# First-phase loads issued one by one behind pieces of the second transform, and five of the last image's tile pairs added by VectorE

## The chip, the cores and the metric

One core of a Trainium2 chip runs the whole program. The metric is the device time of one execution in microseconds, as the median of several runs. A profiled execution is one further run, with its own time. The engines are called PE (TensorE, the matrix engine), PEld (its weight loads), DVE (VectorE), ACT (ScalarE), POOL (GpSimd) and SP (SyncE, which only issues DMA transfers here).

## The reference, cut to what matters

The input `x` has 32 images of 128 channels by 64 x 64 pixels in float32. Three layers follow each other:

```python
x = x + conv(group_norm(x))            # a convolution through 2-D butterfly transforms:
                                       #   transform, product with the transformed weights, transform back
t = to_tokens(x)                       # 32 x 4096 tokens of 128 channels
t = t + attention(layer_norm(t))       # for each image softmax(K^T V) over its 4096 tokens, 128 x 128
t = t + moe(layer_norm(t))             # 8 experts, the best two by router weight, gates renormalised
x = from_tokens(t)
```

In `conv`, `group_norm` has groups of four channels, so every image needs its mean and variance over all 4096 pixels before its transform. In `moe`, each token's result is the sum over experts of gate times expert output; the gates of six of the eight experts are zero, and the kernel computes all eight and weighs them.

## The kernel before, in words

The program has three phases, and one image, or one column of frequencies, at a time goes through each.

**First phase** (about 0 to 980 us): norm and forward transform. Image `b` is loaded in eight pieces of 128 x 512 by SP (`load`, L307), then DVE takes statistics of each piece (`stats`, L315) and joins them (L324). A short exchange between PE (L328, L338), DVE (L333 to L341) and POOL gives the group's mean and the reciprocal of its deviation: POOL's power is L345. From image 4 on DVE then norms the image in four pieces (L358); for the first four images ACT does it (L356). PE transposes the image in four groups, called `pz` (L369), and ACT copies them out (L379). PE multiplies along the width in eight groups, `pv` (L392), and ACT copies (L403). PE multiplies along the height in eight groups, `pf` (L414); the copies `fo` out of the accumulator (L424) are DVE's, except those of groups 3 and 7, which are ACT's. SP stores each copy with two transfers (L432) to the tensor `xf` in HBM. There are three buffers for images (`x`), four accumulators in PSUM for all of `pz`, `pv` and `pf` (`ps`), and four buffers for copies on their way to HBM (`f`).

These stages are pipelined. In the slot `s` of the loop PE does, in turn, pieces of `pz` of image `s`, of `pv` of image `s-1` and of `pf` of image `s-2`.

The order on every engine is written out ahead of time by a small planner, the class `Plan`. Each piece of work is added with an engine, an estimated duration, a due time, what it comes after and which buffers it takes and frees. The planner plays this through, and whenever an engine is free it takes the ready piece with the smallest due time. The order found in this way is the order in which the instructions are issued; each engine then works strictly in that order and waits where data or buffers aren't ready. PE's order in the first phase is that of the code. In the calls of `add`, the due time is in slots of 27.5 us. For the loads it reads:

```python
for k in range(8):
    add(("x", b, k), "SP", 0.45, b - 2 + 0.1 * k, load(b, k), [("pz", b - 3, g) for g in range(4)],
        ("x",) if k == 0 else (), (), 4.0)
for k in range(4):
    add(("bn", b, k), "DVE", 1.4, at + 0.02 * k, stats(b, k), [("x", b, 2 * k), ("x", b, 2 * k + 1), ("nm", b - 2, 3)])
```

So all eight loads of an image become ready when image `b - 3` has been transposed, and one piece of statistics takes two pieces of the image.

The small butterfly matrices of the transforms are built in the same phase (`butterfly`): matrix 1 by DVE at the start, matrices 0 and 2 by POOL during slots 3 to 8, in six levels (`level`, L216 to L222) that each wait for the one before. Their twiddle factors come by SP (L187). `select` (L244 to L250) is a further small piece on POOL. In slots 12 to 15 POOL arranges the weights (L277, L282), PE transposes them (L293) and DVE copies them (L298).

**Second phase** (about 980 to 2650 us): product with the weights, column by column; the change does not touch it.

**Third phase** (about 2650 us to the end): inverse transform, attention and experts, again planned, with one image's experts running beside the next images' earlier stages. An image has 32 tiles of 128 tokens (`NT`), treated in 16 pairs. For each tile and each half of the experts PE makes four experts' outputs, 128 x 512 in one accumulator (`expert`, L1200, three accumulators `pe`). DVE multiplies them by the gates into a tile `tm` (`gated`, L1211); there are two tiles `tm`, one for each pair on its way. POOL adds a pair's sixteen products (`summed`): two additions of 128 x 512 (L1222), one more of the same size (L1223) and two onto the tokens `t` (L1225). PE then transposes four finished tiles back (`back`, L1232), ACT copies (L1238) and SP stores (L1239). For the last image nothing else is left to run beside this. Just before it, DVE works out that image's gates (L1108 to L1152).

Of the kernel before, what the change touches and what calls it, by code (L numbers as in the profile page):

```python
# [12 lines left out]
ALU = mybir.AluOpType  # L13
# [3 lines left out]
P = 128  # L17
# [73 lines left out]
def kernel(  # L91
# [15 lines left out]
    nc = tc.nc  # L107
    B = x.shape[0]
# [11 lines left out]
    pf = dram.tile([n, n, P * n], F32, name="pf")  # L120
# [37 lines left out]
    with ExitStack() as ph1:  # L158
# [9 lines left out]
        made, xs, zs, vs, tile_of = {}, {}, {}, {}, {}  # L168
        on_pe = []

        def add(key, engine, us, at, run, after=(), take=(), free=(), late=0.0):
            after = [made[k] for k in after if k in made]
            if engine == "PE":
                after += on_pe[-1:]
            made[key] = plan.add(engine, us, SLOT * at, run, after, take, free, late)
            if engine == "PE":
                on_pe.append(made[key])
# [5 lines left out]
        def twiddles(m):  # L183
            def run():
                t = tile_of["tw", m] = bp.tile([P, 6, 2, 2, 2, n // 2], F32, tag="tw", name=f"tw{m}")
                for ax in range(2):
                    nc.sync.dma_start(  # L187
                        t[ax * n : (ax + 1) * n].rearrange("p a i j c d -> p (a i j c d)"),
                        tw[m, ax].rearrange("a i j c d -> (a i j c d)").partition_broadcast(n),
                    )  # L190
            return run
# [111 lines left out]
        def load(b, k):  # L303
            def run():
                if k == 0:
                    xs[b] = xp.tile([P, NPIX], F32, tag="x", name=f"x{b}")
                nc.sync.dma_start(xs[b][:, k * 512 : (k + 1) * 512], xv[b][:, k * 512 : (k + 1) * 512])  # L307
            return run

        def stats(b, k):  # L310
            def run():
                if k == 0:
                    tile_of["bs", b] = st.tile([P, 8, 6], F32, name=f"gbs{b}", tag="gbs", bufs=2)
                for j in range(2 * k, 2 * k + 2):
                    nc.vector.bn_stats(tile_of["bs", b][:, j, :], xs[b][:, j * 512 : (j + 1) * 512])  # L315
            return run

        def group_norm(b):
# [116 lines left out]
        def butterfly(m, engine, eng, at, us):  # L435

            before = {1: [], 0: [("b1", 5), "wi", ("nm", 4, 3)], 2: [("b0", 5), "wd"]}[m]
            add(("tw", m), "SP", 0.9, -3.0 if m == 1 else at - 0.3, twiddles(m), before, (), (), 4.0)
            add((f"b{m}", -1), engine, 2 * us / 7, at, unit(m, eng), before)
            for idx in range(6):  # L440
                add((f"b{m}", idx), engine, us, at + 0.01 * idx, level(m, idx, eng), [("tw", m), (f"b{m}", idx - 1)])

        def norm(b):

            at = b - 1
            for k in range(8):
                add(
                    ("x", b, k), "SP", 0.45, b - 2 + 0.1 * k, load(b, k), [("pz", b - 3, g) for g in range(4)],
                    ("x",) if k == 0 else (), (), 4.0,
                )  # L450
            for k in range(4):
                add(("bn", b, k), "DVE", 1.4, at + 0.02 * k, stats(b, k), [("x", b, 2 * k), ("x", b, 2 * k + 1), ("nm", b - 2, 3)])

        def norm_on_pe(b, step):
            if not 0 <= b < B:
                return
            at = b - 0.9
            if step == 0:
                gn = tile_of["gn", b] = group_norm(b)
                add(("ag", b), "DVE", 0.4, at, gn[0], [("bn", b, k) for k in range(4)])  # L460
                add(("g1", b), "PE", 0.3, at, gn[1], [("ag", b)], ("ps",))
                add(("gm", b), "DVE", 0.7, at, gn[2], [("g1", b)])
            else:
                gn = tile_of.pop(("gn", b))
                add(("g2", b), "PE", 0.3, at, gn[3], [("gm", b)])
                add(("gr", b), "DVE", 0.25, at, gn[4], [("g2", b)], (), ("ps",))
                add(("gp", b), "POOL", 0.6 if b >= 4 else 1.6, at, gn[5], [("gr", b)])
                for k in range(4):
                    add(("nm", b, k), *(("DVE", 0.85) if b >= 4 else ("ACT", 1.05)), at + 0.01 * k, gn[6][k], [("gp", b)])
# [34 lines left out]
        norm_on_pe(0, 0)  # L504
        norm_on_pe(0, 1)
        for s in range(B + 2):
            if s + 2 < B:
                norm(s + 2)
            for g in range(4):
                at = s + 0.25 * g  # L510
                if g == min(s, 3) - 1:
                    norm_on_pe(s + 1, 0)
                piece("pz", s, g, at)
                for k in range(2):
                    piece("pv", s - 1, 2 * g + k, at + 0.04 + 0.04 * k)
                if g == min(s, 3) - 1:
                    norm_on_pe(s + 1, 1)
                for k in range(2):
                    piece("pf", s - 2, 2 * g + k, at + 0.12 + 0.07 * k)
            if s == 0:  # L520
                norm_on_pe(1, 0)
                norm_on_pe(1, 1)
            if s == 3:
                butterfly(0, "POOL", nc.gpsimd, 3.2, 4.5)
                add("sel", "POOL", 2.5, 3.5, select, [("nm", 4, 3)])
            if s == 6:
                add("wr", "PE", 0.6, 6.0, weight_rows, [("b0", 5), "sel"], ("ps",))
                add("wd", "DVE", 0.8, 6.0, weight_matrices, ["wr"], (), ("ps",))
                butterfly(2, "POOL", nc.gpsimd, 7.0, 4.5)
                add("wo", "DVE", 1.2, 9.0, output_matrices, [("b2", 5)])  # L530
                add("wm", "SP", 0.5, 10.0, weight_taps, [("b2", 5)], (), (), 4.0)
            if 12 <= s < 16:
                k = s - 12
                add(("wr", k), "POOL", 5.0, s - 0.5, onto_rows(k), ["wm", ("pf", s - 3, 4)], ("f",))
                add(("wt", k), "PE", 1.1, s, rows_turned(k), [("wr", k)], ("ps",))
                add(("we", k), "DVE", 1.25, s, rows_out(k), [("wt", k)], (), ("ps", "f"))
# [4 lines left out]
    with ExitStack() as ph2:  # L541
# [11 lines left out]
        made, tile_of = {}, {}  # L553
# [614 lines left out]
    def experts(b):  # L1168
# [37 lines left out]
        def gated(i, half):  # L1206
# [8 lines left out]
                )  # L1215
            return run

        def summed(j):
            def run():
                tm, lo = tile_of.pop(("tm", b, j)), 2 * j  # L1220
                for k in range(2):
                    nc.gpsimd.tensor_tensor(tm[:, k, 0:4, :], tm[:, k, 0:4, :], tm[:, k, 4:8, :], ALU.add)  # L1222
                nc.gpsimd.tensor_tensor(tm[:, :, 0:2, :], tm[:, :, 0:2, :], tm[:, :, 2:4, :], ALU.add)  # L1223
                for m in range(2):
                    nc.gpsimd.tensor_tensor(t[:, lo : lo + 2, :], t[:, lo : lo + 2, :], tm[:, :, m, :], ALU.add)  # L1225
            return run
# [16 lines left out]
        for g in range(8):  # L1243
            at = s2 + 0.125 * g
            add(b, f"xn{g}", "ACT", 1.7, at - 0.1, normal(g), ["nb"], ("xn",))
            add(b, f"px{g}", "PE", 0.55, at - 0.05, turn(g), [f"xn{g}"], ("tl", "xT"), ("xn",))
            add(b, f"xT{g}", "ACT", 0.6, at - 0.05, turned(g), [f"px{g}"], (), ("tl",))
            for k in range(4):
                i = 4 * g + k
                for half in range(2):  # L1250
                    add(
                        b, f"pe{i}_{half}", "PE", 0.86, at + 0.125 * (2 * k + half) / 8, expert(i, half), [f"xT{g}"],
                        ("pe",), ("xT",) if k == 3 and half else (),
                    )
                    add(
                        b, f"m{i}_{half}", "DVE", 0.7, at + 0.125 * (2 * k + half) / 8, gated(i, half),
                        [f"pe{i}_{half}", "gt"] + ([f"m{i - k % 2}_0"] if k % 2 or half else []), ("tm",) if k % 2 == 0 and half == 0 else (),
                        ("pe",) + (("gate",) if i == NT - 1 and half else ()),
                    )
                if k % 2:  # L1260
                    add(
                        b, f"s{i // 2}", "POOL", 5.45, at + 0.125 * (2 * k + 2) / 8, summed(i // 2),
                        [f"m{i - 1 + a}_{h}" for a in range(2) for h in range(2)], (), ("tm",),
                    )
            add(b, f"st{g}", "PE", 0.55, at + 0.25, back(g), [f"s{2 * g}", f"s{2 * g + 1}"], ("tl",))
            add(b, f"so{g}", "ACT", 0.6, at + 0.25, store(g), [f"st{g}"], (), ("tl",))
# [61 lines left out]
```

## Time and profile before

| what | us |
|---|---|
| median of 3 runs (lowest to highest) | 6242.58 (6241.29 to 6246.91) |
| the profiled execution's own time | 6250.6 |
| its span from first to last instruction | 6248.9 |
| PE busy | 6005.3 (96%) |
| DVE busy | 4200.0 (67%) |
| ACT busy | 3757.1 (60%) |
| POOL busy | 4205.2 (67%) |
| first phase's slots of images 3 to 30 | 824.0, PE busy 783.3 |
| last image's sums on POOL | 6158.1 to 6243.8 |

The page is one profiled execution. Busy time counts instructions at work on an engine; an engine that waits in front of an instruction isn't busy. PE's time is the sum of matrix instructions, with weight loads (PEld) beside it. "Idle before" says how long an engine stood before an instruction and what ended that. The granted clock is the rate that the chip allowed PE, as a share of full speed. Times with a decimal point in the timelines are counted from the start of the span.

### The profile page before, as it was taken

How to read it: one execution, taken by the hardware profiler on the slowest of the kernel's cores; microseconds unless marked ns; L12 is line 12 of the kernel's file. 1: busy time of each engine (PE TensorE's matmuls, PEld its weight loads, DVE VectorE, ACT ScalarE, POOL GpSimd, SP SyncE). 2: the span in 40 equal slices, each digit the busy share in tenths (PEclk: the TensorE clock that was granted, in tenths of full speed). 3: DMA queues.
4: the chain of work that ended last, by engine and by line, in shares of the span. 5: the costliest groups of instructions: out<-in, count | busy, mean ns of one | idle time of the engine just before them, and what ended most of it. 6: DMA issues, size and time to landing. Idle time of an engine off the chain costs nothing. (4 is left out here: it accounts for less than half of the span.)

```text
span 6248.9 us, 218347 instructions
## 1 busy us (share of the span) xinstructions
PE 6005.3 (96%) x94922; PEld 4726.7 (76%) x94922; DVE 4200.0 (67%) x7626; ACT 3757.1 (60%) x7089; POOL 4205.2 (67%) x3780
## 2 busy tenths in 40 slices
PE   7999999999999999889999999999999999999987
PEld 7899998999999999766666666666666666666653
DVE  5555544555555555347878787787878778787876
ACT  6666664555555555466666676667667666766652
POOL 2110005666666666328888888888888888888889
PEclk9999999999999999899999999999999999999999
DMA  5666656666666666622222122222313222221100
GB/s 201 215 216 210 231 192 190 175 171 170 173 174 170 171 172 174 170 77 85 77 67 95 62 93 67 85 78 65 95 62 93 68 85 76 68 94 62 64 21 24
DMA packets 556965, 756.55 MB, mean 121 GB/s; under 512 B 58466, under 2 KB 321892, under 8 KB 551908
## 3 DMA queue, kind: packets, MB, share of 16 engines
q1 hardware_dynamic: 554096, 741.38, 39.7%
q8 instruction: 745, 12.21, 0.9%
q14 instruction: 216, 1.77, 0.1%
q10 hardware_dynamic: 1908, 1.19, 0.1%
HBM read 406.80 MB, written 335.54 MB: 119 GB/s over the span
## 5 line engine op out<-in xcount | busy, mean ns | idle before, releaser
L1200 PE MATMUL pe<-ew_sb,xT 128*128 128x512 f32 x4096 | 1982.4, 601 | 53.2 <-DVE tm L1211 52.8
L1211 DVE TENSOR_TENSOR tm<-pe,oh 128x512 f32<-128x512 f32 x2048 | 1353.4, 684 | 563.4 <-PE pe L1200 419.0
L1222 POOL TENSOR_TENSOR tm<-tm 128x512 f32<-128x512 f32 x1024 | 1306.7, 1291 | 313.1 <-DVE tm L1211 260.7
L1200 PEld LDWEIGHTS pe<-ew_sb,xT 128*128 128x128 f32 x4096 | 691.1, 191 | 523.4 <-issue 327.8
L623 PE MATMUL m<-f,s 128*64 128x64 f32 x32768 | 1070.1, 224 | 6.3 <-POOL s L574 4.6
L612 DVE COPY f<-g 128x1024 f32<-128x1024 f32 x512 | 626.9, 1224 | 664.5 <-PE g L601 664.5
L623 PEld LDWEIGHTS m<-f,s 128*64 128x64 f32 x32768 | 999.1, 138 | 68.3 <-POOL s L574 4.9
L574 POOL COPY s<-l 128x512 f32<-128x512 f32 x512 | 546.9, 1103 | 596.7 <-issue 516.4
L612 ACT COPY f<-g 128x1024 f32<-128x1024 f32 x512 | 518.6, 1013 | 576.6 <-PE g L601 549.3
L1225 POOL TENSOR_TENSOR tk<-tk,tm 128x256 f32<-128x256 f32 x1024 | 759.4, 742 | 80.3
L839 ACT COPY u<-pu 64x512 f32<-64x512 f32 x1024 | 593.5, 580 | 313.7 <-PE pu L829 302.8
L1223 POOL TENSOR_TENSOR tm<-tm 128x512 f32<-128x512 f32 x512 | 652.4, 1274 | 40.2
L829 PEld LDWEIGHTS pu<-qw,r 128*128 128x128 f32 x4096 | 507.2, 198 | 169.1 <-ACT u L839 91.5
L601 PE MATMUL g<-c,wst 9*128 9x128 f32 x16384 | 608.0, 284 | 4.7 <-ACT f L612 3.5
L829 PE MATMUL pu<-qw,r 128*128 128x128 f32 x4096 | 526.2, 284 | 62.5 <-ACT u L839 55.4
L345 POOL TENSOR_TENSOR grstd<-gms,mhalf 128x1 f32<-128x1 f32 x32 | 17.7, 553 | 790.0 <-DVE gms L341 752.8
L601 PEld LDWEIGHTS g<-c,wst 9*128 9x128 f32 x16384 | 509.3, 187 | 40.7 <-ACT f L612 4.5
L414 PE MATMUL pf<-ph,v 128*128 128x128 f32 x4096 | 497.4, 280 | 22.3 <-issue 15.9
L576 POOL TENSOR_SCALAR s<-l 128x512 f32<-128x512 f32 x256 | 510.3, 1993 | 0.0
L414 PEld LDWEIGHTS pf<-ph,v 128*128 128x128 f32 x4096 | 471.9, 193 | 33.8 <-issue 17.4
L1238 ACT COPY so<-po 128x512 f32<-128x512 f32 x256 | 150.9, 589 | 572.7 <-issue 413.1
L884 DVE BATCH_NORM_STATS2 bs<-tk 128x6 f32<-128x128 f32 x2048 | 447.9, 279 | 57.0 <-ACT tk L915 44.9
(165 smaller groups left out, 8486.1 us busy)
## 6 DMA issues: line engine op xcount, KB each, us to landing
xf<-f SPq DMA_DIRECT2D x512, 256.0 KB, 3.9
l<-xf SPq DMA_DIRECT2D x1024, 128.0 KB, 3.3
pf<-o SPq DMA_DIRECT2D x1024, 128.0 KB, 3.2
r<-pf SPq DMA_DIRECT2D x512, 256.0 KB, 4.7
x<-in_x_dram SPq DMA_DIRECT2D x256, 256.0 KB, 5.4
y<-in_x_dram SPq DMA_DIRECT2D x32, 2048.0 KB, 8.2
out_dram<-so SPq DMA_DIRECT2D x256, 256.0 KB, 2.0
tw<-in_tw_dram SPq DMA_DIRECT2D x6, 384.0 KB, 6.0
```

Of the source, the lines that this page charges most:

```text
L414: nc.tensor.matmul(pl[:, j * P : (j + 1) * P], vs[b][:, 8 * g + j, :], ph.rearrange("h r m -> h (r m)"), start=True, stop=True,)
L574: nc.gpsimd.tensor_copy(dst, src)
L601: nc.tensor.matmul(pg[g // 2][:, g % 2, m * P : (m + 1) * P], wst[rows, 16 * half + 4 * t + m, :], c[rows].rearrange("r h k -> r (h k)"), ...
L612: copy(f.rearrange("i m (g o) -> i m g o", g=2), tile_of["g", w, half, t][k].rearrange("i g (o m) -> i m g o", o=4))
L623: nc.tensor.matmul(ps[hh * n : (hh + 1) * n, q, :], s[:, h].rearrange("i k b -> i (k b)")[:, B * r : B * r + n], f[:, h, r, :], start=(r = ...
L829: nc.tensor.matmul(ps[:, k, :], rs[b, e][:, k * P : (k + 1) * P], qw.rearrange("w r m -> w (r m)"), start=True, stop=True,)
L839: nc.scalar.copy(u[r * n : (r + 1) * n, :, oh * n + 8 * e : oh * n + 8 * e + 8], ps[oh * n : (oh + 1) * n, :, r * n : (r + 1) * n].rearran ...
L1200: nc.tensor.matmul(ps, tile_of["xT", b, i // 4][:, i % 4, :], ew_sb[:, es, :].rearrange("d e c -> d (e c)"), start=True, stop=True,)
L1211: nc.vector.tensor_tensor(tile_of["tm", b, i // 2][:, i % 2, es, :], tile_of.pop(("pe", b, i, half)).rearrange("p (e c) -> p e c", c=P), t ...
L1222: nc.gpsimd.tensor_tensor(tm[:, k, 0:4, :], tm[:, k, 0:4, :], tm[:, k, 4:8, :], ALU.add)
L1223: nc.gpsimd.tensor_tensor(tm[:, :, 0:2, :], tm[:, :, 0:2, :], tm[:, :, 2:4, :], ALU.add)
L1225: nc.gpsimd.tensor_tensor(t[:, lo : lo + 2, :], t[:, lo : lo + 2, :], tm[:, :, m, :], ALU.add)
```

## The change

In the first phase, the statistics are added to the plan piece by piece, eight for an image, each after the one before. From image 4 on, load `k` of image `b` comes after load `k - 1` and after piece `k` of the height transform `pf` of image `b - 4`, and is added to the plan inside the loop over the slot's groups. The butterflies on POOL, but not their twiddle loads, get a due time later by 99 slots, and `select` gets the due time 99.

In the third phase, for the last image alone, five of the sixteen tile pairs (3, 6, 9, 12 and 15) are neither multiplied into `tm` nor added by POOL. Instead DVE takes each expert's output from the accumulator, multiplies it by the gate of the token and adds it onto `t` with one instruction per expert: four for each half, sixteen for a pair.

```diff
@@ stats
-                for j in range(2 * k, 2 * k + 2):
-                    nc.vector.bn_stats(tile_of["bs", b][:, j, :], xs[b][:, j * 512 : (j + 1) * 512])
+                nc.vector.bn_stats(tile_of["bs", b][:, k, :], xs[b][:, k * 512 : (k + 1) * 512])
@@ butterfly
             add(("tw", m), "SP", 0.9, -3.0 if m == 1 else at - 0.3, twiddles(m), before, (), (), 4.0)
+            at += 99 if engine == "POOL" else 0
             add((f"b{m}", -1), engine, 2 * us / 7, at, unit(m, eng), before)
@@
+        def piece_of_image(b, k):
+
+            add(
+                ("x", b, k), "SP", 0.45, b - 2 + 0.1 * k, load(b, k),
+                [("pz", b - 3, g) for g in range(4)] + [("x", b, k - 1), ("pf", b - 4, k)],
+                ("x",) if k == 0 else (), (), 4.0,
+            )
+
         def norm(b):
 
             at = b - 1
+            for k in range(8) if b < 4 else ():
+                piece_of_image(b, k)
             for k in range(8):
-                add(
-                    ("x", b, k), "SP", 0.45, b - 2 + 0.1 * k, load(b, k), [("pz", b - 3, g) for g in range(4)],
-                    ("x",) if k == 0 else (), (), 4.0,
-                )
-            for k in range(4):
-                add(("bn", b, k), "DVE", 1.4, at + 0.02 * k, stats(b, k), [("x", b, 2 * k), ("x", b, 2 * k + 1), ("nm", b - 2, 3)])
+                add(("bn", b, k), "DVE", 0.7, at + 0.01 * k, stats(b, k), [("x", b, k), ("nm", b - 2, 3), ("bn", b, k - 1)])
@@ norm_on_pe
-                add(("ag", b), "DVE", 0.4, at, gn[0], [("bn", b, k) for k in range(4)])
+                add(("ag", b), "DVE", 0.4, at, gn[0], [("bn", b, k) for k in range(8)])
@@ the loop over slots
-            if s + 2 < B:
-                norm(s + 2)
+            if s == 0:
+                norm(2)
...
                 for k in range(2):
                     piece("pf", s - 2, 2 * g + k, at + 0.12 + 0.07 * k)
+                    if 4 <= s + 2 < B:
+                        piece_of_image(s + 2, 2 * g + k)
+            if 3 <= s + 2 < B:
+                norm(s + 2)
...
-                add("sel", "POOL", 2.5, 3.5, select, [("nm", 4, 3)])
+                add("sel", "POOL", 2.5, 99, select, [("nm", 4, 3)])
@@ experts
+        def weighed(i, half):
+
+            def run():
+                ps = tile_of.pop(("pe", b, i, half))
+                for e in range(4):
+                    nc.vector.scalar_tensor_tensor(
+                        t[:, i, :], ps[:, e * P : (e + 1) * P], tile_of["gate", b][:, i, 4 * half + e : 4 * half + e + 1],
+                        t[:, i, :], ALU.mult, ALU.add,
+                    )
+            return run
+
+
+        direct = (3, 6, 9, 12, 15) if b == B - 1 else ()
...
                     add(
-                        b, f"m{i}_{half}", "DVE", 0.7, at + 0.125 * (2 * k + half) / 8, gated(i, half),
-                        [f"pe{i}_{half}", "gt"] + ([f"m{i - k % 2}_0"] if k % 2 or half else []), ("tm",) if k % 2 == 0 and half == 0 else (),
+                        b, f"m{i}_{half}", "DVE", 1.45 if i // 2 in direct else 0.7, at + 0.125 * (2 * k + half) / 8,
+                        weighed(i, half) if i // 2 in direct else gated(i, half),
+                        [f"pe{i}_{half}", "gt"] + ([f"m{i - k % 2}_0"] if k % 2 or half else []),
+                        ("tm",) if k % 2 == 0 and half == 0 and i // 2 not in direct else (),
                         ("pe",) + (("gate",) if i == NT - 1 and half else ()),
                     )
-                if k % 2:
+                if k % 2 and i // 2 in direct:
+                    made[b, f"s{i // 2}"] = made[b, f"m{i}_1"]
+                elif k % 2:
                     add(
                         b, f"s{i // 2}", "POOL", 5.45, at + 0.125 * (2 * k + 2) / 8, summed(i // 2),
```

## The prediction

> **What bounds the kernel now.** I read the page first: TensorE (PE) is busy for 96% of the span, so time can only come from where PE waits, or from a stretch that another engine sets. The busy digits show two such stretches that the change touches: the first phase (0 to 980 us, PE digit mostly 9 but not full) and the last 90 us, where PE is at 7 and POOL at its highest.
>
> For the first phase I cut the time at the first transposition of each image (PE L369) and asked for the windows. Columns: window, its length, then busy time of PE, PEld, DVE, ACT, POOL, granted clock, DMA share, GB/s. The first row is images 3 to 30, 28 slots; then the slot of image 7, a clean one (10), and 11.
> ```profile
> 89.67:913.67 824.00, 783.33 (x18966) 748.43 (x18965) 456.41 (x647) 531.26 (x732) 81.43 (x227) 0.99 0.63 216
> 204.88:242.78 37.90, 28.03 (x679) 26.52 (x678) 15.30 (x28) 21.05 (x31) 23.25 (x71) 0.92 0.82 268
> 301.43:328.83 27.40, 27.30 (x679) 26.20 (x677) 16.02 (x24) 18.89 (x26) 0.55 (x1) 1.00 0.68 233
> 328.83:358.47 29.64, 27.55 (x679) 26.38 (x677) 16.77 (x24) 18.89 (x26) 5.01 (x14) 1.00 0.63 211
> ```
> A clean slot lasts 27.40 us and PE fills it; the average is 824.0 / 28 = 29.43. PE is bound in a clean slot, and something holds it in the others. The waits of DVE and of SP's queue in the same 824 us (total, times, longest) name candidates:
> ```profile
> DVE gbs L315 <- DMA x<-in_x_dram: 81.8, 84, 2.7
> ```
> ```profile
> SPq L307 <- PE pz L369: 146.2, 26, 6.2
> SPq L432 <- DVE gmv L324: 110.0, 27, 11.7
> ```
> DVE stands in the statistics (L315) waiting for loads; SP stands in front of a load until the transpositions have freed its buffer, and stores (L432) wait until the whole run of statistics is over. The timeline of slot 11 shows how that reaches PE:
> ```profile
> 327.49 2.76 SPq L307 DMA_DIRECT2D x<-in_x_dram  x5
> 328.34 1.28 DVE L315 BATCH_NORM_STATS2 gbs<-x 128x6 f32<-128x512 f32 x2
> ...
> 333.20 2.05 DVE L315 BATCH_NORM_STATS2 gbs<-x 128x6 f32<-128x512 f32 x3 [2.46 <-DMA x<-in_x_dram]
> 336.40 1.32 DVE L315 BATCH_NORM_STATS2 gbs<-x 128x6 f32<-128x512 f32 x2 [1.15 <-DMA x<-in_x_dram]
> 336.48 1.27 PE L414 MATMUL pf<-ph,v 128*128 128x128 f32 x10 [1.98 <-issue]
> ...
> 337.63 1.21 DVE L424 COPY f<-pf 128x1024 f32<-128x1024 f32 x1
> ```
> The eight statistics run from 328.34 to 337.7 with nothing between them. The copy of the finished accumulator (L424) stands behind them, the four accumulators fill, and PE stops for 1.98 us.
>
> Slot 7 has another cause, in the timelines of POOL and PE:
> ```profile
> 240.78 0.55 POOL L345 TENSOR_TENSOR grstd<-gms,mhalf 128x1 f32<-128x1 f32 x1
> ```
> ```profile
> 242.73 1.94 PE L369 MATMUL pz<-ident,x 128*128 128x128 f32 x8 [8.64 <-issue]
> ```
> The power for the norm (L345) could have run at 223.7, after L341, but stands behind all six butterfly levels of 3.8 us on POOL.
>
> The end is in the chain of waits: from 6158.08 it is one POOL sum after another.
> ```profile
> 6158.08 1.27 POOL tm L1222
> 6159.39 1.27 POOL tm L1222
> 6160.74 1.28 POOL tm L1223
> ...
> 6162.09 0.74 POOL tk L1225
> ...
> 6162.90 0.72 POOL tk L1225
> ```
> Later sums start every 5.40 us (6174.44, 6179.84, 6185.24); the last adds at 6243.08. DVE is busy for only 40 of these 86 us, so POOL alone sets the end.
>
> **What the Trainium skill says.** "GPSIMD Engine Reference", section "Key points": POOL shares its SBUF interfaces with VectorE, and instructions with two SBUF inputs or in a 2-port mode contend. The trace agrees: L1152, two SBUF inputs, takes 424 ns at least and 1374 at the median, while those with one input in PSUM and one in SBUF stay flat beside a busy POOL (below: min/median/max). The new DVE instruction is of this second kind.
> ```profile
> L1211 DVE TENSOR_TENSOR tm<-pe,oh x2048: 661/682/694, 2771.1 to 6235.8; 128x512 f32<-128x512 f32 x187
> ```
> "VectorE: DVE Perf Modes", section "The DRAIN you can't avoid": a semaphore between dependent DVE instructions costs nothing extra. Here L1109 to L1112, each waiting for the one before, start 0.34 to 0.46 us apart at 0.42 us each; I allow 0.04. "TensorE: Matmul & The Clock Gate", Part 1: PE falls to half clock after an idle window of about 3.4 us. Here it also does after 2.84 us (slot 17: granted 0.90), so a stall costs more than its length.
>
> **The change, part by part.**
>
> Loads and statistics (first phase). From image 4 on, load k is issued behind piece k of `pf` instead of as soon as the buffer is free. The numbers stay: 256 loads, 256 statistics of 0.69 us. In the order that the planner makes, a slot's SP queue now reads load, two stores, load, two stores; the first load's wait for PE is over by then, since the four `pz` it needs lie in the slot before, so no store stands behind it. On DVE the run of eight becomes two, one, three and two, with copies between. What remains to be waited for: load 1, issued behind the stores of f0, has to land before the copy of f2. In slot 11 that copy would be due some 6.5 us after f0's; a load took 5.5 us at the median in the steady part. I cost the wait at nothing, covered by that margin and by the four accumulators; beyond it every microsecond goes to PE.
>
> What can be won: 28 clean slots are 767.2; the 36 extra matmuls for the weights add 32 x 0.13 + 0.5, some 4.6. 824.0 - 767.2 - 4.6 = 52.2 us are stalls and half clock.
>
> POOL's butterflies get a due time 99 later, so L345 goes ahead of what is left: before level 5 of the first and before level 3 of the second. In the second, twiddles landed at 217.9, so three levels end at 229.4; power 0.55 and four norms of 0.75 end at 233, and PE needs the image at 234.1. Slots 7 and 8 lie 10.5 and 2.0 over clean; I take 12 of these 12.5. The twiddle loads keep their place behind a slot's last store. `select` moves ahead of the first butterfly: 3.2 us on an otherwise idle POOL.
>
> The other 39.7 us are spread over 26 slots, 1.5 each. I take three quarters, 30, as the run of statistics is the visible cause in most, but weight rows (slots 12 to 15) still borrow a store buffer and DMA stays at 0.63. First phase: -42. Bounds: -25 (half of each) and -55 (all, and the 2.8 us of stalls in slot 2, where image 4's statistics also lose their run).
>
> Last image. Pairs 3, 6, 9, 12 and 15 leave POOL: -5 x 5.40 = -27.0. On DVE each loses four products of 0.69 and gets 16 multiply-adds of 128x128. The trace has none with this shape; L775, the same operation on 128x512, takes 686 ns, as much as L1211, and a 128x128 copy out of PSUM (L994) 292. I take 0.31 + 0.04 = 0.35, a pair 5.6 us. Between direct pairs DVE has two ordinary ones, 5.5, so 11.1 us per three pairs against POOL's 10.8. Followed through the trace's start (pair 0 at 6156.7, buffers back at 6163.6, 6169.0): direct pair 3 from 6167.1 to 6172.7, pair 4 just in time for POOL at 6174.4, and after that DVE falls behind by 0.3 each group; the last sum, of pair 14, ends at 6218.0 instead of 6244.6, and pair 15 on DVE at 6217. So -26; -27 if an instruction costs 0.30, -20 at 0.42. PE's output transpositions move a place in its queue; each still waits for its own sum.
>
> Sum: 6250.6, the profiled execution's own time (span 6248.9 and 1.7 around it), - 42 - 26 = 6182.6. The shown median is 8.0 below that execution, so **6175**.
>
> **Rivals.** (a) The forecast, 75%.
>
> (b) The stalls have another cause, such as four accumulators shared by three stages, and little but the end is won, with part of the butterfly's 12: -26 - 8 = 6209. For it: PE also stalls in slots where DVE's waits for loads are short. Against: clean slots have the same work in the same accumulators. 16%.
>
> (c) Slower: loads arrive just in time no longer. Three groups of statistics now stand in front of copies, each behind a load issued only some 6 us earlier. If loads land at 9 to 10 us, each group holds the copies beyond the margin, say 4.5 us a slot: 28 x (4.5 - 52.2 / 28) - 26 = +48, 6290. It decides from 3.2 us lost per slot, where 28 x (3.2 - 1.86) - 26 = +12. Against: 5.5 us median with bursts of eight, which go. 5%.
>
> (d) The multiply-adds contend with POOL after all, through the [P,1] scalar: at 1.3 us each a pair takes 21, five groups 5 x 26 = 130 instead of 86 us, +44 against -42: no change. 4%.
>
> The range holds (a) with its bounds and reaches to (b): 6160 to 6209; left out are (c), (d), the farther half of (b) and the ends of (a), some 2 in 10. Smallest difference to be told from none is 0.2%, 12.5 us: faster 0.91, same 0.04, slower 0.05.
>
> **What would show it.** Right: in the windows, slots near 27.4 to 28 and the 28-slot stretch at 782; DVE's wait for x under 30 us; SP L307's wait for `pz` gone; no gap before PE L369 at the second butterfly; eleven POOL sums in the end's chain without gaps. Wrong: PE gaps remaining behind L315, a DVE multiply-add over 0.42 us, or the chain's end on DVE.

## The result, and the profile after

Over paired runs the changed kernel takes 6182.57 us (median of 4 runs, 6176.46 to 6192.43) against 6244.74 (6241.29 to 6249.73): a ratio of 0.9901 with a 95% interval of [0.9884, 0.9918], 62 us less. Its profiled execution has an own time of 6179.1 us and a span of 6177.3; the kernel before had 6250.6 and 6248.9. Line numbers of the first phase are one lower than before (L307 stays, L315 is L314, L424 is L423, L432 is L431); the expert products L1200 are L1209, the gated ones L1211 are L1220, POOL's sums L1222 to L1225 are L1245 to L1248. All ratios compare fast executions: one slow execution of each of two experiments below (tail_only, 17,860 us at a granted clock of 0.32, and burst_between, 6531 us) is left out.

From landmarks in both traces: the first transposition of image 3 comes 2.4 us earlier, that of image 31 comes 50.3 us earlier, and the last image, from DVE's first product by a gate to the end of the span, takes 75.0 us in place of 92.2, so 17.2 less. What lies between moved by 4 us; that is no effect, as the same changed kernel took 9 us more there in its second profile (after_again, below).

Windows of the changed kernel (length, then busy PE, PEld, DVE, ACT, POOL, granted clock, DMA share, GB/s): images 3 to 30, then the slots of images 7 and 10.
```profile
87.31:863.34 776.03, 769.62 (x18966) 739.13 (x18965) 456.75 (x651) 530.91 (x732) 85.20 (x227) 1.00 0.69 231
197.65:225.97 28.32, 27.62 (x679) 26.34 (x678) 17.00 (x26) 19.87 (x30) 19.22 (x54) 1.00 0.78 246
282.07:309.40 27.33, 27.22 (x678) 26.20 (x677) 16.04 (x23) 18.90 (x26) 0.55 (x1) 1.00 0.70 234
```
A slot is now 27.7 us on average where a clean one is 27.33, and slot 7 fell from 37.90 to 28.32. Of the 48.0 us won in these 28 slots, PE's own busy time gives back 13.7 (783.3 to 769.6 for the same matrix instructions; the mean granted clock was 0.99 before and is 1.00 now), the rest are stops.

Waits in the same stretch of the changed kernel (total us, times, longest):
```profile
DVE gbs L314 <- DMA x<-in_x_dram: 108.7, 56, 3.6
```
```profile
SPq L431 <- DVE f L423: 388.1, 154, 6.5
...
SPq L307 <- PE pv L391: 2.9, 8, 0.7
```
SP's wait for `pz` is gone, as it should be. But DVE's wait for loads has *grown*, from 81.8 to 108.7 us, while the slots became clean. So that wait is not by itself the price. What PE itself waited for says more. First the kernel before, 28 slots:
```profile
PE pf L414 <- issue: 13.7, 9, 2.8
...
PE pz L369 <- issue: 8.6, 1, 8.6
...
PE pv L392 <- DVE f L424: 8.1, 11, 1.4
...
PE pv L392 <- issue: 4.5, 7, 1.7
...
PE pf L414 <- DVE f L424: 2.1, 7, 1.0
```
and the changed one:
```profile
PE pv L391 <- issue: 1.1, 2, 0.7
...
PE pv L391 <- DVE f L423: 0.8, 1, 0.8
...
PE pf L413 <- issue: 0.3, 2, 0.2
```
The 8.6 is slot 7's missing norm. Of the rest, only about 10.6 us (with 0.4 for ACT's copies) were waits for a copy out of an accumulator; 18.2 us stand under "issue", a wait for nothing that the view can name. Of these, 0.8 and 1.4 us are left. (ACT's copies `z` held PE for at most 0.8 us in any of these kernels; they are left out here and in the table below.)

**What "issue" was.** The page of the kernel before has a line that bears on it, among its DMA queues (packets, MB, share of the 16 engines' span):
```profile
q8 instruction: 745, 12.21, 0.9%
```
PE has 94,922 matrix instructions and as many weight loads; divided by 745 packets that is 255 instructions a packet, of 16 KB each: this queue brings TensorE its own program, a packet about every 5 us. The Trainium skill, "Runtime: NRT & Kernel Launch", section "Instruction fetch mechanics", describes such blocks of 256 instructions, fetched over a DMA queue of the engine's own, and calls the cost mostly hidden. Here it was not: 18.2 us of these 28 slots. Slot 17 of the kernel before, with its longest stop but slot 7's: the DMA queues between 505.5 and 511.6 us and in the microsecond after that, then PE's and DVE's timelines.
```profile
q1 hardware_dynamic: 962, 1.75, 94.7%
```
```profile
q1 hardware_dynamic: 187, 0.34, 94.7%
q8 instruction: 1, 0.02, 5.5%
```
```profile
514.13 1.23 PE L414 MATMUL pf<-ph,v 128*128 128x128 f32 x4 [2.84 <-issue]
```
```profile
516.89 1.22 DVE L424 COPY f<-pf 128x1024 f32<-128x1024 f32 x1 [0.16 <-PE pf L414]
```
SP had issued five loads from 506.55 on. Between 505.5 and 511.6 us the sixteen DMA engines are 95% busy with data and no packet of instructions starts. PE runs dry at 511.3, a packet starts at 511.7 and takes 0.9, PE resumes at 514.13. It resumes 2.8 us *before* the copy that the prediction would have blamed, so it did not wait for that copy. (Starts and durations of single packets are from the trace's packet records.)

For the last image, the longest pieces of the changed kernel's chain of waits near its end (start, us, engine), and the new instruction and the waits in that stretch:
```profile
6154.54 2.59 PE pe L1209 x6
6160.45 1.96 PE pe L1209 x4
6162.84 1.73 PE pe L1209 x4
6164.58 1.26 POOL tm L1246
...
6173.86 0.59 ACT so L1261
```
```profile
L1232 DVE SCALAR_TENSOR_TENSOR tk<-pe,oh,tk x80: 341/351/354, 6114.6 to 6173.0; 128x128 f32<-128x128 f32 x80
```
```profile
POOL tm L1245 <- DVE tm L1220: 10.1, 10, 2.2
DVE tm L1220 <- PE pe L1209: 8.9, 24, 1.1
...
PE pe L1209 <- DVE tk L1232: 3.8, 10, 0.5
```
POOL is no longer a row of sums without a gap: the chain alternates between PE's expert products and DVE's multiply-adds of the direct pairs (pieces of 0.36 us, too short for the list above; one row of them fills 6157.19 to 6160.32), it reaches POOL only in its last 13 us, and all three engines wait for each other in turn.

### The profile page after: what moved, and what is told of

It reads as the page before. It is cut to its first block, busy times and chain, and to the rows that moved or that the text cites. A ratio compares the mean times of both kernels' runs of the same rounds, so it can differ in the third digit from the quotient of the medians.

```text
span 6177.3 us, 218388 instructions
## 1 busy us (share of the span) xinstructions
PE 5988.3 (97%) x94922; PEld 4714.0 (76%) x94922; DVE 4213.0 (68%) x7686; ACT 3759.2 (61%) x7089; POOL 4187.1 (68%) x3755
## 5 line engine op out<-in xcount | busy, mean ns | idle before, releaser
L1209 PE MATMUL pe<-ew_sb,xT 128*128 128x512 f32 x4096 | 1984.6, 601 | 44.8 <-DVE tm L1220 40.6
L1220 DVE TENSOR_TENSOR tm<-pe,oh 128x512 f32<-128x512 f32 x2028 | 1341.2, 684 | 535.0 <-PE pe L1209 422.4
L1245 POOL TENSOR_TENSOR tm<-tm 128x512 f32<-128x512 f32 x1014 | 1296.3, 1293 | 314.6 <-DVE tm L1220 263.4
L1209 PEld LDWEIGHTS pe<-ew_sb,xT 128*128 128x128 f32 x4096 | 691.0, 191 | 518.7 <-issue 333.1
L1248 POOL TENSOR_TENSOR tk<-tk,tm 128x256 f32<-128x256 f32 x1014 | 753.4, 743 | 79.5
L838 PEld LDWEIGHTS pu<-qw,r 128*128 128x128 f32 x4096 | 503.6, 196 | 170.1 <-ACT u L848 92.2
L610 PEld LDWEIGHTS g<-c,wst 9*128 9x128 f32 x16384 | 510.9, 187 | 40.6 <-ACT f L621 4.5
```

What stands on the lines that cost most here:

```text
L610: nc.tensor.matmul(pg[g // 2][:, g % 2, m * P : (m + 1) * P], wst[rows, 16 * half + 4 * t + m, :], c[rows].rearrange("r h k -> r (h k)"), ...
L838: nc.tensor.matmul(ps[:, k, :], rs[b, e][:, k * P : (k + 1) * P], qw.rearrange("w r m -> w (r m)"), start=True, stop=True,)
L1209: nc.tensor.matmul(ps, tile_of["xT", b, i // 4][:, i % 4, :], ew_sb[:, es, :].rearrange("d e c -> d (e c)"), start=True, stop=True,)
L1220: nc.vector.tensor_tensor(tile_of["tm", b, i // 2][:, i % 2, es, :], tile_of.pop(("pe", b, i, half)).rearrange("p (e c) -> p e c", c=P), t ...
```

## The experiments

The theories. **A**: the run of eight statistics on DVE holds the copies (the prediction's). **B**: the burst of eight loads does the harm, as SP stands in front of it with stores behind (B1) or by the 2 MB that it puts ahead of the stores (B2). **D**: it works by two roads through data at once, late loads and late stores. **C**: it holds back TensorE's instruction packets. **E**: in the last image PE sets the pace between direct pairs and DVE in them. "Slots" is the time from image 3's first transposition to image 31's; the two last columns are PE's waits in it, from the same view as above. These three columns are of one profiled execution each. How much such a figure varies can be read from kernels with the same first phase: 824.0 and 824.2 us for the old one, 776.0 to 782.0 for the changed one in five profiles.

| kernel | ratio to before [95%] | slots 3-30, us | PE "issue", us | PE for copies, us |
|---|---|---|---|---|
| before | 1 | 824.0 | 18.2 (+8.6 norm) | 10.6 |
| the changed kernel | 0.9901 [0.9884, 0.9918] | 776.0 | 1.4 | 0.8 |
| before_f6 | 1.0001 [0.9992, 1.0009] | 817.5 | 17.5 (+8.0 norm) | 7.8 |
| bfly_only | 0.9982 [0.9975, 0.9990] | 811.7 | 16.2 | 10.1 |
| burst_between | 0.9986 [0.9978, 0.9993] | 812.0 | 25.9 | 3.8 |
| between_f6 | 0.9981 [0.9974, 0.9989] | 804.6 | 23.1 | none |
| burst_late | 0.9950 [0.9934, 0.9967] | 789.0 | 13.8 | none |
| run_of_8 | 0.9940 [0.9926, 0.9955] | 787.3 | 5.0 | 6.1 |
| p1_only | 0.9930 [0.9914, 0.9947] | 779.2 | 3.0 | 1.7 |
| spare_burst | one run, 6240.99 us | 819.4 | 30.9 | 6.6 |
| tail_only | 0.9978 [0.9966, 0.9991] | 824.2 | 20.3 (+8.9 norm) | 7.3 |
| after_again | 0.9898 [0.9883, 0.9912] | 777.0 | 1.5 | 1.2 |
| four | 0.9903 [0.9888, 0.9918] | 782.0 | 4.3 | 0.9 |
| quarter | 0.9896 [0.9879, 0.9912] | 776.5 | 1.8 | 1.1 |

**The two halves alone.** p1_only has the new first phase and the old last image, by the edit below; tail_only has the first phase of the kernel before and the last image of the changed one.
```diff
 p1_only, from the changed kernel
-        direct = (3, 6, 9, 12, 15) if b == B - 1 else ()
+        direct = ()
```


> The whole first-phase part of the change, with the last image's sums all on POOL as before. Theory A (the run of eight statistics on DVE held the accumulators' copies, and the spread loads break it up): the slots of images 3 to 30 last 776 us as in the changed kernel (before: 824), the time falls by some 50 us, to 0.992 of before; the last image's stretch from its first product to the end stays at 92 us. Rival T (most of the measured gain comes from the end): only 35 to 40 us.

> The five direct pairs alone, first phase as before. Theory E (PE and DVE take turns at setting the pace in the last image: ordinary pairs at PE's 0.86 us a half, direct ones at DVE's 1.54): the last image's stretch is 75 us as in the changed kernel against 92, so -17 us, 0.9973. The prediction's own step would give -26, 0.9958.

Measured: p1_only's span is 44.8 us shorter, between the 50 of A and the 35 to 40 of T, and its interval, 33 to 54 us, holds both. tail_only's last image takes 74.9 us in place of 92.2, 17.3 less; its total is some 13 us lower at the median. That is as theory E has it, and the prediction's 0.9958 lies outside the interval. The ratios leave 0.7% and 0.22%, together 0.92%, beside the 0.99 [0.82, 1.16] of the whole: the halves add up.

**Which part of the first phase.** run_of_8 keeps the single loads, but puts all eight statistics in one run behind the last load; burst_between keeps the old burst, but spreads the statistics between the copies. Both have the late butterflies and the old last image. The edits show what each piece comes after; burst_between also moves the calls that add the loads and the statistics to the plan.
```diff
 run_of_8
-  stats(b, k), [("x", b, k), ("nm", b - 2, 3), ("bn", b, k - 1)]
+  stats(b, k), [("x", b, 7), ("nm", b - 2, 3), ("bn", b, k - 1)]
 burst_between
-  load(b, k), [("pz", b - 3, g) for g in range(4)] + [("x", b, k - 1), ("pf", b - 4, k)]
+  load(b, k), [("pz", b - 3, g) for g in range(4)]
-  stats(b, k), [("x", b, k), ("nm", b - 2, 3), ("bn", b, k - 1)]
+  stats(b, k), [("x", b, k), ("nm", b - 2, 3), ("bn", b, k - 1), ("pf", b - 4, k)]
```


> First phase as in the changed kernel, loads spread behind pieces of pf, but all eight statistics of an image wait for its last load, so that they stand in one run on DVE again; last image as before. Theory A (the run on DVE is what stops PE): gaps return, in each slot once behind the statistics, though the loads have landed: 5.5 us of run instead of 5.5 + 3 of waits, so some 0.5 us a slot, the 28 slots at 785 to 800 us. Theory B (the burst of loads, and stores held up in SP's queue behind a load's wait for the transpositions, are what stops PE): no gaps, 776 us as with the whole first-phase part.

> Loads all eight as soon as the buffer is free, as before the change, but each piece of statistics held behind a piece of pf, so that DVE has copies between them; butterflies with the late due time; last image as before. Theory A: the gaps go although loads come in a burst and SP waits in front of them: 28 slots at 776 to 782 us. Theory B: the gaps stay, 28 slots at some 812 us (824 less the butterfly's 12).

With single loads the run of eight costs little: 787.3 us, inside A's range but near its lower end, some 8 us over p1_only, and 4.9 of its 6.1 us of copy waits are one stop. With the burst, spread statistics win nothing beyond the late butterflies (812.0 against bfly_only's 811.7), as B has it. So A falls as the main cause: most of the 32 us between bfly_only and p1_only come with the burst. The table shows something that the totals hide: spreading the statistics did cut PE's wait for copies, from 10.1 to 3.8, but its "issue" rose from 16.2 to 25.9. Less waiting for copies, more "issue", and no time won.

**The late butterflies alone**, in the kernel before:
```diff
             add(("tw", m), "SP", 0.9, -3.0 if m == 1 else at - 0.3, twiddles(m), before, (), (), 4.0)
+            at += 99 if engine == "POOL" else 0
...
-                add("sel", "POOL", 2.5, 3.5, select, [("nm", 4, 3)])
+                add("sel", "POOL", 2.5, 99, select, [("nm", 4, 3)])
```


> The kernel before with the late butterflies and select alone. By the prediction's step: slots 7 and 8 lose 12 of their 12.5 us over a clean slot, the 28 slots take about 812 us, total about 6234, ratio 0.998. If the pieces are not independent (slot 7 runs into the stall of the load burst once POOL is out of the way) only about 8 are won: 816 us, ratio 0.9987.

Slots 3 to 30 take 811.7 us, 12.3 less, as the first expectation has it; but slots 7 and 8, the only ones that it speaks of, lost 8.1 us (67.3 to 59.3), as the second has it, and the other 4 us are no more than such figures vary. With the norm in time, slot 7 still takes 31.1 us, with two stops under "issue" and one for a copy in it. The single loads then took off most of what was left there (56.7 in the changed kernel).

**How the burst harms: by SP, by stores?** burst_late issues the whole burst behind piece 0 of `pf`, where nothing of `pz` is left to wait for; before_f6 gives the kernel before six store buffers in place of four.
```diff
 burst_late, from p1_only
-  [("x", b, k - 1), ("pf", b - 4, k)]
+  [("x", b, k - 1), ("pf", b - 4, 0)]
-  stats(b, k), [("x", b, k), ("nm", b - 2, 3), ("bn", b, k - 1)]
+  stats(b, k), [("x", b, k), ("nm", b - 2, 3), ("bn", b, k - 1), ("pf", b - 4, min(7, k + 1))]
 before_f6, from before
-  fp = ph1.enter_context(tc.tile_pool(name="fp", bufs=4))
-  plan = Plan({"x": 3, "ps": 4, "f": 4}, quick=True)
+  fp = ph1.enter_context(tc.tile_pool(name="fp", bufs=6))
+  plan = Plan({"x": 3, "ps": 4, "f": 6}, quick=True)
```


> The first phase of the changed kernel, the old last image; only the order of the loads differs: all eight loads of an image are issued in one go behind piece 0 of the second transform (four, a store, two, a store, two in the SP queue), and the statistics keep nearly the changed kernel's place between the copies. So the eight loads form a burst as before, but SP does not stand in front of the first of them waiting for pz, because those transpositions lie a slot back. Theory B1 (the harm was SP standing in front of the load, with finished stores queued behind it): no stalls, slots 3 to 30 about 779 us as with single loads, total about 6204, ratio 0.993. Theory B2 (the harm is the burst of 2 MB itself, which delays the stores issued behind it and so the store buffers): stalls stay, slots 3 to 30 at 800 to 812 us, total about 6228 to 6238, ratio 0.997 to 0.9986. SP's wait for pz gone in either case.

> The kernel before with six store buffers f in place of four in the first phase, nothing else (burst of eight loads, SP's wait for pz, run of eight statistics, early butterflies and old last image all stay). Theory B (late stores reach PE through store buffers that come free too late, in either form B1 or B2): the copies have a buffer although two stores are late, most of the 36 us outside the butterfly slots goes: slots 3 to 30 at 785 to 800 us, total 6210 to 6225, ratio 0.994 to 0.997. If the loads' late arrival in front of the run of statistics were what counts, more store buffers change nothing: 824 us, ratio 1.000.

Neither form of B is met: burst_late lies between its two values, at 789.0, and six buffers change nothing in the total (ratio 1.0001). It is the "issue" column of these two, 13.8 and 17.5 us, that points to the packets. A stop in before_f6, DVE's timeline and then PE's, looks like the run of statistics at work:
```profile
768.50 2.03 DVE L315 BATCH_NORM_STATS2 gbs<-x 128x6 f32<-128x512 f32 x3 [3.67 <-DMA x<-in_x_dram]
```
```profile
770.82 0.60 PE L414 MATMUL pf<-ph,v 128*128 128x128 f32 x4 [1.82 <-issue]
```
DVE waits 3.67 us for a load and PE stops. Yet PE resumes at 770.82, while DVE is still in its run (its next copy starts at 772.35), and an instruction packet has come in between, from 768.6 to 769.6. So PE did not wait for that copy: the late load and the stop only lie side by side.

**With all waits for data covered.** between_f6 is burst_between with six store buffers: late loads meet statistics that can wait, late stores meet free buffers. D and C part here.

```diff
 from burst_between
-  fp = ph1.enter_context(tc.tile_pool(name="fp", bufs=4))
-  plan = Plan({"x": 3, "ps": 4, "f": 4}, quick=True)
+  fp = ph1.enter_context(tc.tile_pool(name="fp", bufs=6))
+  plan = Plan({"x": 3, "ps": 4, "f": 6}, quick=True)
```


> Burst_between (old burst of loads, statistics piece by piece between the copies, late butterflies, old last image) with six store buffers in place of four, nothing else. Here neither the statistics nor the store buffers can hold the copies for long, although loads and stores are late. Theory D (the burst does its harm by two roads at once, late loads in front of the run of statistics and late stores in front of the copies; six buffers alone left the first road, statistics between the copies alone left the second): both roads are closed, slots 3 to 30 at 780 to 790 us, total about 6205 to 6212, ratio 0.994. Theory C (most of what PE still loses waits for no data at all: TensorE's own instructions come by DMA, in packets of 16 KB about every 5 us, and these stand behind the burst; in burst_between 23 of 28 stops of PE end 1.2 to 1.7 us after such a packet has come): stops stay, slots 3 to 30 at 800 to 812 us, total 6225 to 6237, ratio 0.997 to 0.9986, and PE resumes 1.2 to 1.7 us after a packet in most of them.

```profile
PE pf L413 <- issue: 14.4, 12, 2.5
...
PE pv L391 <- issue: 8.7, 11, 2.2
```
No wait of PE for a copy is left, and PE still stops for 23.1 us; the slots take 804.6. In the trace's packet records, 19 of 22 stops of over 0.25 us (21.1 of 23.4 us) end 1.2 to 1.7 us after an instruction packet has come; a packet comes every 5.4 us, so an arbitrary moment lies in such a window of 0.5 us in 9 of 100 cases. D falls, and C's forecast is met.

**The cause alone, added to the good kernel.** spare_burst is p1_only with five store buffers and, in each slot, six more loads into a tile that nothing reads.
```diff
+        spare = xp.tile([P, 6 * 512], F32, tag="spare", name="spare", bufs=1)
...
+                for k in range(6):
+                    nc.sync.dma_start(spare[:, k * 512 : (k + 1) * 512], xv[b][:, k * 512 : (k + 1) * 512])
...
+        add(("spare", s + 2), "SP", 3.0, s + 0.75, burst(s + 2), [("x", s + 2, 7)])
```


> The changed kernel's first phase with its single loads, the old last image and five store buffers, and besides in every slot from image 4 on a burst of six loads of 256 KB from x into a spare tile that nothing reads, issued by SP behind the image's last load. No instruction waits for the spare tile. Theory C (TensorE's instruction packets stand behind the burst): stops of PE come back, most of them ending 1.2 to 1.7 us after a packet, the longest distance between two packets is again over 8 us in many slots, slots 3 to 30 at 795 to 815 us against 779 without the spare burst. Theory D (only data that arrive or leave late hurt): the first loads of the next image and one slot's last stores are late by the burst's 5 us, which the statistics' place and five buffers mostly cover: 779 to 790 us, and where PE stops, it resumes at the end of a copy and not behind a packet.

```profile
PE pv L391 <- issue: 18.7, 17, 2.6
...
PE pf L413 <- issue: 12.2, 12, 2.9
...
PE pv L391 <- DVE f L423: 6.6, 10, 1.4
```
```profile
SPq L431 <- DMA spare<-in_x_dram: 36.9, 91, 2.6
```
Transfers whose data nobody reads bring the stops back: 30.9 us under "issue" in place of 3.0, slots of 819.4 us in place of 779.2, and 27 of 35 stops (30.8 of 36.7 us) end 1.2 to 1.7 us behind a packet. They are not wholly without a waiter, as was expected: SP stood in front of stores and loads until a spare transfer had landed, 36.9 us in the line above and 16.7 more in front of loads. Loads and stores were late by that too, and 6.6 us of PE's waits are for copies. The slots lie 4 us above C's range and 29 above D's.

Where the stops stand settles it. PE's records in the kernel before, numbered in order of their start (matrix instructions, weight loads and the 929 of its sequencer between them), are 190,773, which is 256 for each of the 745 packets. Every "issue" stop of slots 3 to 30 except the norm's stands at number 193 or 194 in its block of 256: 16 of 16 in the kernel before, 24 of 24 in burst_between, 23 of 23 in between_f6, 29 of 29 in spare_burst, and the 4 that the changed kernel has left. No wait of PE for a named copy stands there. So these stops come where the next packet of instructions is due, whatever PE and the other engines are doing with data at the time.

**The last image.** after_again is the changed kernel once more; four has pairs 3, 7, 11 and 15 direct; in quarter only pair 15 is, and in every other pair DVE adds the odd tile's second half straight onto `t`, so that POOL makes one addition less (the planner's durations are set to match, not shown).
```diff
 four
-        direct = (3, 6, 9, 12, 15) if b == B - 1 else ()
+        direct = (3, 7, 11, 15) if b == B - 1 else ()
 quarter
-        direct = (3, 6, 9, 12, 15) if b == B - 1 else ()
+        direct = (15,) if b == B - 1 else ()
+        last = b == B - 1
+        def alone(i, half):
+            return i // 2 in direct or (last and i % 2 and half)
...
-                        weighed(i, half) if i // 2 in direct else gated(i, half),
+                        weighed(i, half) if alone(i, half) else gated(i, half),
...
-                for k in range(2):
+                for k in range(1 if last else 2):
                     nc.gpsimd.tensor_tensor(tm[:, k, 0:4, :], tm[:, k, 0:4, :], tm[:, k, 4:8, :], ALU.add)
```


> The changed kernel once more, as it is, on the same chip and beside the two variants of its last image. Ratio to before 0.990 as shown; from the last image's first product to the end of the span 74.9 us, give or take 1.

> The changed kernel with four direct pairs (3, 7, 11 and 15) in place of five, so that POOL has twelve sums in place of eleven. Prediction's reading (POOL sets the end): one sum of 5.40 us more, the last image takes 80.3 us in place of 74.9. Theory E (between direct pairs PE sets the pace, some 3.55 us for an ordinary pair, and DVE in direct ones, 6.16 us for a pair; POOL has waits left): 12 x 3.55 + 4 x 6.16 = 67.2 us of products and multiply-adds in place of 69.9, so the last image takes about 72.2 us. Total: +5 or -3 against after_again.

> The changed kernel with another division of the last image: only pair 15 is direct as a whole; in every other pair DVE adds four of the sixteen products straight onto t (the odd tile's second half) and POOL the other twelve, with one addition of 128 x 512 less, some 4.0 us a sum. By theory E's prices a pair then costs DVE 3 x 0.69 + 1.54 = 3.61, PE some 3.55 to 4.0 and POOL 4.0, with no stretch in which one of them waits out the others: 16 x 4.0 + 4 = 66 to 70 us for the last image in place of 74.9, total 5 to 8 us under after_again. If DVE alone set the pace and each multiply-add out of PSUM costs more when products lie between (theory F), nothing is won: 74 to 76 us.

From the last image's first product to the span's end: 75.0 us for the changed kernel in both its profiles, 75.0 for four, 69.4 for quarter. Four misses both expectations. Its products and multiply-adds did get shorter, 68.8 us for 71.0, near the 2.7 less that E expects; but POOL's twelfth sum then ends last, and PE's final transposition waits 4.4 us for it:
```profile
PE po L1255 <- POOL tk L1248: 4.4, 1, 4.4
```
With five direct pairs DVE's last multiply-add ends 0.6 us after POOL's last sum, with four it ends 1.4 us before it: they lie on the two sides of one crossing. Quarter's last image is what E expects: up to pair 15 no engine waits out the others' direct pairs, and the stretch of products is 65.4 us. Its total misses the 5 to 8 us expected: 6186.2 against 6188.4 for after_again, which cannot be told apart. So the 5.5 us rest on its one profile, and only by its last image is it the best of these.

## Why the prediction was right or wrong

The total was met, 62 us less where 68 were forecast, and in profiled executions 71.5 less; but its two terms were off to opposite sides, by 8 and 9 us, and cancelled. That the total came so near is luck.

- **First phase, -42: measured -50.** Slots 7 and 8, taken at 12, gave 10.6. The step that failed is "I take three quarters, 30, as the run of statistics is the visible cause in most". The other 26 slots gave 37.3 of their 39.7, nearly all, since the single loads took away the burst, and with it the late instruction packets (18.2 us of "issue" to 1.4). The waits for copies, which the run of statistics was to explain, were the smaller part, some 10 us. The reading that misled is the timeline of slot 11, in the prediction's own fence: PE resumes at 336.48, the copy that was said to hold it starts only at 337.63, and the wait is marked "issue", not L424.
- **The loads' margin, costed at nothing:** right. DVE waits 108.7 us for loads, yet PE stood only 0.8 us for a copy. But "DVE's wait for x under 30 us" was the wrong sign to look for: a wait with nothing needed behind it may grow.
- **L345 ahead of the butterflies:** right. Slot 8 begins without a gap before its first transposition, and `pz`'s 8.6 us are gone.
- **Last image, -26: measured -17.2.** "Between direct pairs DVE has two ordinary ones, 5.5" is the step that failed. It took DVE's busy time for the pace and never asked PE, which needs 3.45 us for a pair's eight matmuls (the chain of the changed kernel has such a stretch at 6111.09). PE did not get far enough ahead during the direct pairs: it waited ten times, 3.8 us, until one of them freed an accumulator; whether a fourth accumulator would help was not tried. Cut at DVE's first instruction of each kind, two ordinary pairs took 6.95 to 7.46 us and the first three 12.2; a direct pair took 6.07 to 6.15, not 5.6, as a multiply-add takes 351 ns and starts 387 ns after the one before (median). The row read for that margin, L1109 to L1112, is not one in which each waits: L1111 starts 0.34 us after L1110, which takes 0.42; the other two steps are 0.46 and 0.45. A group of three is then 13.0 us or more, beyond POOL's 10.8, and POOL's sums no longer set the end; the eleven sums without gaps, named as a sign of being right, did not come. In sum 40.6 us of ordinary pairs and 30.4 of direct ones make the 71.0 us of the stretch.
- **Rivals.** (b), "the stalls have another cause", was true of the cause, but not of what follows from it: the change happened to remove that cause too. (c) fell: loads that landed late held no copy for long. (d) fell: the multiply-adds stay between 341 and 354 ns beside a busy POOL.

How far ahead PE asks for a packet can be read from the same numbering: in the kernel before and the changed one, after the first 50 us, none started more than 300 instructions before the place where it is due, and from 3300 to 6000 us, where the DMA engines are busy for 24% and 23% of the time, the medians are 258 and 256: about one block. Still open: why a burst behind piece 0 of `pf` costs some 10 us (789.0 against 779.2) and one behind the last `pz` some 25 (804.6, with six store buffers); the place in the slot matters, and no run here varied it by itself. The 13.7 us by which the same matrix instructions took longer in the kernel before were not tried by themselves.

## What to carry to other kernels

When PE stops and the profile names no releaser, compare when it resumes with the end of the work you suspect, and look at the DMA queue that carries its instructions, and at whether the stops keep to one place in each block of 256 instructions. In this kernel PE needed a packet about every 5 us, and bulk transfers issued at one go held it up, even those whose data nobody read. Spread such transfers over the time that they have. When work is moved from the engine that sets the end to another, price each remaining stretch on every engine that takes part, the one that seems to have time left included.

## What was unexpected of the hardware

Instruction packets and data share the DMA engines closely enough that 1.5 to 2 MB at one go stop TensorE for up to 2.9 us, and 1.2 to 1.7 us pass between the end of the packet and the first matmul after such a stop. In the kernel before, 15 of its 28 stops of over 0.25 us end in this way (18.5 of 35.9 us), in the changed one two of five. Loads and stores also landed later in the kernel with the burst: in the middle of the first phase a store after 4.3 us and a load after 5.4 (medians), and after 3.4 and 4.6 in the changed kernel.
